# A two-layer graph network on one core: steps re-ordered, block sums a step later, layer 0's edges loaded 1 MB at a time

## The chip, the cores and the metric

The kernel runs on one core of a Trainium2 chip. The metric is the device time of one execution in microseconds (us); ten executions of the kernel before gave a median of 2218.96 us, from 2216.50 to 2221.39. Engines are named as the profile names them: PE (matrix multiply), PEld (its weight loads), DVE (vector), ACT (activations and copies), POOL (here: issues the gathers) and SP (here: issues most other transfers). SBUF is the on-chip memory; PSUM is the small memory in banks that PE writes its results to.

## The reference, cut to what matters

N = 6250 nodes, E = 106250 edges sorted by their destination, D = 256 features, all fp32. Both layers use the same `src`, `dst` and `edge_attr`.

```python
def layer_0(x, src, dst, edge_attr):
    msg = relu(x[src] + edge_attr)
    agg = segment_sum(msg, dst, num_segments=N)
    h = x + (x + agg)
    f = bn1(h)
    f = gelu(f @ W1.T + b1)
    f = f @ W2.T + b2
    return bn2(h + f)

def layer_1(x1, src, dst, edge_attr):
    h = gelu((x1[src] + edge_attr) @ W1m + b1m)
    agg = segment_sum(h @ W2m + b2m, dst, N) / maximum(deg, 1.0)
    u = gelu(agg @ W1u + b1u) @ W2u + b2u
    return layernorm(x1 + u, gamma, beta)

x1  = layernorm(x  + layer_0(x, ...))
out = layernorm(x1 + layer_1(x1, ...))
```

Each layer reads one row of 256 floats per edge from a table of nodes, at an address given by `src`, adds the edge's own row, applies a function, and sums the results by destination.

## The kernel before, in words

**Edges.** They are cut into 831 tiles of 128. Eight tiles make a *span* (104 spans; the last has seven tiles, the last of these ten edges). A span has two groups `g` of G = 4 tiles, a group two pairs of tiles that start at `q` = 0 and 2. A pair of 128 x 512 floats fills one PSUM bank.

**Nodes.** They are cut into 25 blocks of 256 (the last has 106). As edges are sorted by destination, a span touches one or two blocks. Blocks 22, 23 and 24 are complete after spans 98, 102 and 103.

**Layer 1 turned round.** (x1[src] + e) @ W1m + b1m is computed as proj[src] + e @ W1m, where proj = x1 @ W1m + b1m is made once per node. Layer 0 also computes z = e @ W1m for group 0 of each span and stores it in DRAM (`zst`, L1032 to L1041); layer 1 loads that and computes the product for group 1 alone. W2m @ W1u is joined to one matrix w12 (`join_weights`, L1056 to L1080).

**One span's way.** `load_edges` (L755) loads each group's 512 KB, three spans ahead (AHEAD). `gather` (L768, its transfer L772) issues eight indirect transfers on POOL, one per tile, into one of RING = 5 buffers `ring`. `lifted` (L804) copies two tiles of edges into a PSUM bank on ACT, and `add_to_gathered` (L816, DVE) adds them to the gathered rows. `activated` (L824, ACT) applies relu or gelu. `one_hots` (L833, DVE) makes 128 x 32 matrices of zeros and ones that say which of 32 consecutive node slots an edge belongs to; `into_slots` (L855, PE) multiplies by them, so that a span becomes 128 partial rows, and ACT copies these to `sums` (L861). `slot_nodes` (L842) makes the second matrix of zeros and ones, from slots to nodes, and `into_blocks` (L879, PE) adds the partial rows to the block's accumulator `acc`; in layer 0 it also counts the degrees, one matmul and one DVE addition for each block part (L886, L890). `turned` (L779) transposes two tiles of edges on PE into the one bank of the pool `eaP` (L785), and ACT copies them to `eaT` (L790); `product` (L793, PE L798) multiplies them by W1m.

**A block's way.** When its last span is in, a generator is started: `nodes_0` or `nodes_1`. Each step of the loop calls `advance` (L912), which lets every running generator do one more stage, up to its next `yield`. `nodes_0` (L918 to L987): scale and copy of acc (fT L924, hT L929); matmuls L935 and gelu L940; matmuls L948 and L953, additions L958 and L959, normalization (L898 to L905), store of x1; transposes L970 and copy L973; matmuls L979, addition L983 and the store of the block's rows of `proj`. `nodes_1` (L1082 to L1142): the mean by degree (L1086 to L1090), two stages of matmuls L1100 with L1105 and gelu L1109, then L1115 to L1136 with matmuls L1125, and the last normalization with the store of `out`.

**Order.** It is written out by hand; no scheduler moves anything. The engines run their own instruction streams in the order in which the code issues them, held only by data and buffers. `step_0(v)` and `step_1(v)` work on three spans at once: they gather span v, add and activate span u = v-1, and sum span w = v-2. SP issues the loads and stores, in order. PSUM has 8 banks: accP 2, slotP 1, eaP 1, workP 4, the last shared by lifted, product, degrees and nodes. Before the first gather, a check of `dst` computes `astray` (L751); POOL waits for it.

**Between the layers** stand the loads of layer 1's first three spans, the two last steps of layer 0, then `join_weights`, then the rest of the node stages; layer 1's first gather needs all of `proj`.

Of the kernel before, what the change touches and what calls it, by code (L numbers as in the profile page):

```python
# [17 lines left out]
G = 4  # L18
# [484 lines left out]
def kernel(  # L503
# [224 lines left out]
    with (  # L728
        tc.tile_pool(name="state", bufs=1) as state,
        tc.tile_pool(name="edges", bufs=(AHEAD + 1) * GROUPS) as ep,  # L730
# [4 lines left out]
        tc.tile_pool(name="eaP", bufs=1, space=bass.MemoryType.PSUM) as pse,  # L735
# [12 lines left out]

        ps = work()
# [5 lines left out]
        def load_edges(v, g):  # L755
            counts = tiles_of(v, g)
            ea = ep.tile([P, G, D], F32, name="ea")
            for j, k, n in runs(counts):
                r0 = (v * SPAN + g * G + j) * P
                nc.sync.dma_start(  # L760
                    out=ea[:n, j:k, :],
                    in_=edge_attr[r0 : r0 + (k - j - 1) * P + n, :].rearrange(
                        "(j p) d -> p j d", p=n
                    ),
                )
            return ea
# [12 lines left out]
        def turned(v, g, q, ea):  # L779

            pair = tiles_of(v, g)[q : q + 2]
            pe = pse.tile([P, 2, KC, P], F32, name="eaP")
            for j, n in enumerate(pair):
                for k in range(KC):
                    nc.tensor.transpose(  # L785
                        pe[:, j, k, :n], ea[:n, q + j, k * P : (k + 1) * P], ident[:n, :n]
                    )
            eaT = hp.tile([P, 2, KC, P], F32, name="eaT", bufs=3)
            for j, k, n in runs(pair):
                nc.scalar.copy(eaT[:, j:k, :, :n], pe[:, j:k, :, :n])  # L790
            return pair, eaT
# [55 lines left out]
        def into_slots(v, width):  # L847

            counts = tiles_of(v, 0) + tiles_of(v, 1)
            hot, r = hots.pop(v), rings[v % RING]  # L850
            ps = pss.tile([P, D + 1], F32, name="slotP")
            for i in range(PAIR):
                for j in range(i, len(counts), PAIR):
                    n, q = counts[j], j // PAIR
                    nc.tensor.matmul(  # L855
                        ps[q * SLOTS : (q + 1) * SLOTS, :width],
                        lhsT=hot[:n, j, :], rhs=r[:n, j, :width],
                        start=(i == 0), stop=(i == PAIR - 1 or j + 1 == len(counts)),
                    )
            sums[v] = hp.tile([P, D + 1], F32, name="sums")  # L860
            nc.scalar.copy(sums[v][:, :width], ps[:, :width])  # L861

        def into_blocks(v, acc, opened, degs=None):

            its, hot, lo0 = sums.pop(v), hot2s.pop(v), window[v][0]
            for b, lo, hi in parts(v):
                at, fresh = hot[:, lo - lo0 : hi - lo0], b not in acc
                begins = opened(b) if fresh else False
                if begins:

                    lo, hi = b * SB, b * SB + shape(b)[0]
                    at = hp.tile([P, SB], F32, name="hot3")[:, : hi - lo]
                    nc.vector.tensor_scalar(  # L873
                        at, ramp[:, : hi - lo], float(lo), node_of[:, v : v + 1],
                        op0=ALU.add, op1=ALU.is_equal,
                    )
                cols = slice(lo - b * SB, hi - b * SB)
# [6 lines left out]
                if degs is not None:  # L884
                    ps = work()
                    nc.tensor.matmul(  # L886
                        ps[:1, 0, : hi - lo], lhsT=its[:, D : D + 1], rhs=at,
                        start=True, stop=True,
                    )
                    nc.vector.tensor_add(degs[b][:, cols], degs[b][:, cols], ps[:1, 0, : hi - lo])  # L890
            return [b for b in sorted(acc) if last_span[b] == v]
# [20 lines left out]
        def advance():  # L912

            for gen in list(running):
                if next(gen, "done") == "done":
                    running.remove(gen)


        def nodes_0(b, acc, xb, deg):
# [11 lines left out]
            ps = work()  # L931
# [12 lines left out]
            ps = work()  # L944
# [14 lines left out]
            nc.vector.tensor_add(ps, ps, bn2_b[:n, None, :].to_broadcast([n, H, D]))  # L959
            x1 = npool.tile([P, SH, D], F32, name="x1")  # L960
            normalized(x1, ps, n, H)
# [3 lines left out]

            x1T = npool.tile([P, KC, SB], F32, name="x1T")
            ps = work()
# [8 lines left out]
            ps = work()  # L976
# [14 lines left out]
        def load_0(v):  # L991
            for b in range(blocks):
                if first_span[b] == v:
                    _, H, n = shape(b)
                    xbs[b] = npool.tile([P, SH, D], F32, name="xb", bufs=4)
                    nc.sync.dma_start(out=xbs[b][:n, :H, :], in_=rows_of(x, b))
            for g in range(GROUPS):
                eas[v, g] = load_edges(v, g)

        def opened_0(b):  # L1000
# [10 lines left out]
            degs[b] = npool.tile([1, SB], F32, name="degs", bufs=3)  # L1011
            nc.vector.memset(degs[b], 0.0)
            return False

        def step_0(v):
# [66 lines left out]
        def nodes_1(b, acc, x1, deg):  # L1082
# [13 lines left out]
            for i in range(0, UC, 2):  # L1096
                ps = work()
# [6 lines left out]
                for o in (i, i + 1):  # L1104
# [3 lines left out]
                    )  # L1108
                    nc.scalar.activation(  # L1109
# [4 lines left out]
            ps = work()  # L1114
# [7 lines left out]
            ps = work()  # L1122
# [6 lines left out]
            nc.vector.tensor_add(ps[:n, :H, :], ps[:n, :H, :], r[:n, :H, :])  # L1129
            mv = normalized(None, ps, n, H)  # L1130
            for h in range(H):
                nc.vector.scalar_tensor_tensor(
                    ps[:n, h, :], ps[:n, h, :], mv[:n, h, 0:1], row["L1_gnn_gamma"][:n, :],
# [3 lines left out]
                    ps[:n, h, :], ps[:n, h, :], mv[:n, h, 1:2], y[:n, h, :],  # L1137
                    op0=ALU.mult, op1=ALU.add,
                )
            yield  # L1140
            normalized(y, ps, n, H)
# [4 lines left out]
        def load_1(v):  # L1146
# [10 lines left out]
            eas[v, 0] = ep.tile([P, G, D], F32, name="ea")  # L1157
            nc.sync.dma_start(out=eas[v, 0].rearrange("p j d -> p (j d)"), in_=zst[v])
            eas[v, 1] = load_edges(v, 1)
# [4 lines left out]

        def step_1(v):
            u, w = v - 1, v - 2
# [4 lines left out]
            if 0 <= w:  # L1171
                slot_nodes(w)
            some = 0 <= u < V
            if some:
                first = turned(u, 1, 0, eas[u, 1])
                for q in (0, 2):
                    add_to_gathered(u, 0, q, lifted(u, 0, q, eas[u, 0]))
            if 0 <= w:
                into_slots(w, D)
            if some:  # L1180
                second = turned(u, 1, 2, eas[u, 1])
                add_to_gathered(u, 1, 0, product(*first))
                activated(u, 0, AF.Gelu)
                one_hots(u)
            full = into_blocks(w, acc_1, opened_1) if 0 <= w else []
            if some:
                add_to_gathered(u, 1, 2, product(*second))
                activated(u, 1, AF.Gelu)
            advance()
            for b in full:  # L1190
                gen = nodes_1(b, acc_1.pop(b), x1s.pop(b), degs_1.pop(b))
                next(gen)
                running.append(gen)
# [3 lines left out]
        for v in range(V):  # L1197
            step_0(v)
        for v in range(AHEAD):
            load_1(v)  # L1200
        step_0(V)
        step_0(V + 1)
        join_weights()
        while running:
            advance()
        for v in range(V + 2):
            step_1(v)
        while running:
            advance()
# [5 lines left out]

# [55 lines left out]
```

## Time and profile before

| what | value |
|---|---|
| median of 10 executions | 2218.96 us (2216.50 to 2221.39) |
| the profiled execution | 2217.28 us, its span 2215.4 us |
| PE, PEld busy | 1856.5 us (84%), 1452.1 us (66%) |
| DVE, ACT busy | 1440.3 us (65%), 1347.2 us (61%) |
| POOL busy | 1576.8 us (71%) |
| moved by DMA | 531.79 MB, mean 240 GB/s |

The page of the profile lists busy times, a picture of the span in 40 slices, the DMA queues, the chain of work that ended last, and the costliest groups of instructions. In a group's row the part behind the bar is the busy time, the mean of one instruction in ns, and the idle time of the engine just before these instructions with what ended most of it. In the waits a row reads: engine, tile and line, what it waited for, us in total, times, longest.

### The profile page before, as it was taken

To read this page: it belongs to the slowest core of one execution; us is meant where nothing else is said; L and a number is where in the kernel's file an instruction comes from. 1 tells how busy PE (TensorE), PEld (TensorE's weight loads), DVE (VectorE), ACT (ScalarE), POOL (GpSimd) and SP (SyncE) were. 2 spreads that over 40 slices of the span, in tenths; PEclk is the share of its full clock that TensorE was granted. 3 is DMA by queue.
4 is the path that set the end of the run, shared out by engine and by line. 5 is a ranking of instruction groups with operands and counts; after the bars stand their busy time and mean duration, and the time that the engine had idled before them with its cause. 6 is when DMAs were issued, how large, how long until landed. Compare 5 with 4: busy or idle time off the path is not lost.

```text
span 2215.4 us, 38426 instructions
## 1 busy us (share of the span) xinstructions
PE 1856.5 (84%) x11916; PEld 1452.1 (66%) x11916; DVE 1440.3 (65%) x4130; ACT 1347.2 (61%) x2143; POOL 1576.8 (71%) x1671
## 2 busy tenths in 40 slices
PE   3889989989899899889758878888888888888885
PEld 2667767767777777667546666666666666666664
DVE  4567666666666766667435676667667667666665
ACT  1566666666667666667534666566566566666664
POOL 3777777777777777777357777777777777777770
PEclk9999999999999999999879999999999999999998
DMA  7888988889889889888456677667667766776650
GB/s 231 267 276 281 286 276 284 278 283 288 274 280 291 277 274 292 279 274 272 147 179 226 213 226 235 224 213 241 215 218 230 236 214 215 240 231 211 221 183 19
DMA packets 313740, 531.79 MB, mean 240 GB/s; under 512 B 37989, under 2 KB 233144, under 8 KB 313400
## 3 DMA queue, kind: packets, MB, share of 16 engines
q1 hardware_dynamic: 231190, 307.82, 41.3%
q0 software_dynamic: 79744, 217.71, 33.3%
q10 hardware_dynamic: 2594, 3.71, 0.5%
q8 instruction: 100, 1.64, 0.3%
q14 instruction: 112, 0.92, 0.1%
HBM read 455.34 MB, written 73.75 MB: 239 GB/s over the span
## 4 chain that ended last, share of the span: by engine, by line
PE 22%; DVE 10%; ACT 7%; DMA 6%; issue 5%; POOL 1%; DVEq 0%; POOLq 0%
PE workP L798 11%; DMA ring<-proj,src_sb 6%; PE workP L1100 4%; PE acc L879 3%; ACT ring L824 3%; PE eaP L785 2%; ACT uT L1109 2%; DVE ring L816 2%; ACT eaT L790 2%; DVE hot L833 1%; DVE inv L1087 1%; DVE uT L1105 1%; POOL ring L772 1%; DVE stats L898 1%; PE slotP L855 1%
## 5 line engine op out<-in xcount | busy, mean ns | idle before, releaser
L772 POOL DMA_INDIRECT ring<-proj,src_sb x831 | 788.4, 949 | 299.2 <-issue 150.2
L772 POOL DMA_INDIRECT ring<-in_x_dram,src_sb x831 | 786.5, 946 | 286.0 <-issue 134.1
L798 PE MATMUL workP<-w1m_sb,eaT 128*128 128x256 f32 x3324 | 819.4, 391 | 7.6 <-DVE ring L816 6.4
L816 DVE TENSOR_TENSOR ring<-workP,ring 128x512 f32<-128x512 f32 x832 | 546.8, 685 | 429.2 <-ACT workP L809 157.3
L824 ACT ACTIVATE ring<-ring 128x1024 f32<-128x1024 f32 x418 | 439.6, 1052 | 553.1 <-DVE ring L816 453.9
L798 PEld LDWEIGHTS workP<-w1m_sb,eaT 128*128 128x128 f32 x3324 | 617.5, 195 | 102.1 <-DVE ring L816 17.2
L785 PE MATMUL eaP<-ident,ea 128*128 128x128 f32 x1662 | 266.2, 284 | 150.6 <-ACT eaT L790 150.4
L785 PEld LDWEIGHTS eaP<-ident,ea 128*128 128x128 f32 x1662 | 193.0, 143 | 263.7 <-ACT eaT L790 237.5
L809 ACT COPY workP<-ea 128x512 f32<-128x512 f32 x624 | 345.0, 589 | 0.0
L855 PE MATMUL slotP<-ring,hot 128*32 128x257 f32 (+1 forms) x3324 | 269.6, 390 | 62.7 <-ACT ring L824 41.7
L879 PE MATMUL acc<-hot,sums 128*128 128x160 f32 (+19 forms) x1360 | 227.3, 295 | 75.9 <-DVE hot L873 46.9
L790 ACT COPY eaT<-eaP 128x512 f32<-128x512 f32 x416 | 242.6, 583 | 63.9 <-PE eaP L785 62.8
L879 PEld LDWEIGHTS acc<-hot,sums 128*128 128x128 f32 x1360 | 203.7, 195 | 106.0 <-DVE hot L873 47.1
L833 DVE TENSOR_SCALAR hot<-ramp,slot 128x32 f32<-128x32 f32 x1662 | 266.9, 262 | 0.0
L855 PEld LDWEIGHTS slotP<-ring,hot 128*32 128x32 f32 x3324 | 109.6, 109 | 156.7 <-ACT ring L824 75.9
L1032 DVE COPY z<-workP 128x512 f32<-128x512 f32 x104 | 71.9, 691 | 90.8 <-PE workP L798 90.6
L900 ACT ACTIVATE mv<-mv,eps 128x2 f32<-128x2 f32 (+1 forms) x75 | 22.2, 295 | 136.6 <-DVE mv L899 136.3
L1100 PE MATMUL workP<-fT,w 128*128 128x256 f32 (+1 forms) x400 | 94.1, 379 | 0.7 <-DVE fT L1090 0.7
L900 ACT ACT_TABLE_LOAD x73 | 93.7, 1283 | 1.3
L1125 PE MATMUL workP<-w2u_sb,uT 128*128 128x256 f32 (+1 forms) x392 | 89.0, 379 | 3.4 <-ACT uT L1109 3.4
L1100 PEld LDWEIGHTS workP<-fT,w 128*128 128x128 f32 x400 | 76.0, 193 | 11.4 <-PE workP L1100 1.1
L1125 PEld LDWEIGHTS workP<-w2u_sb,uT 128*128 128x128 f32 (+1 forms) x392 | 74.1, 190 | 13.9 <-ACT uT L1109 3.8
(109 smaller groups left out, 1425.6 us busy)
## 6 DMA issues: line engine op xcount, KB each, us to landing
ea<-in_edge_attr_dram SPq DMA_DIRECT2D x310, 512.0 KB
zst<-z SPq DMA_DIRECT2D x104, 512.0 KB
ea<-zst SPq DMA_DIRECT2D x104, 512.0 KB
ring<-in_x_dram,src_sb POOLq DMA_INDIRECT x831
ring<-proj,src_sb POOLq DMA_INDIRECT x831
xb<-in_x_dram SPq DMA_DIRECT2D x24, 256.0 KB
x1d<-x SPq DMA_DIRECT2D x24, 256.0 KB
proj<-y SPq DMA_DIRECT2D x24, 256.0 KB
```

What stands on the lines that cost most here:

```text
L772: nc.gpsimd.indirect_dma_start(out=rings[v % RING][:n, g * G + j, :D], out_offset=None, in_=table, in_offset=bass.IndirectOffsetOnAxis(ap= ...
L785: nc.tensor.transpose(pe[:, j, k, :n], ea[:n, q + j, k * P : (k + 1) * P], ident[:n, :n])
L790: nc.scalar.copy(eaT[:, j:k, :, :n], pe[:, j:k, :, :n])
L798: nc.tensor.matmul(ph[:n, j, :], lhsT=eaT[:, j, k, :n], rhs=w1m_sb[:, k, :], start=(k == 0), stop=(k == KC - 1),)
L809: nc.scalar.copy(ps[:n, j:k, :], of[:n, q + j : q + k, :])
L816: nc.vector.tensor_add(r[:n, at + j : at + k, :D], ps[:n, j:k, :], r[:n, at + j : at + k, :D])
L824: nc.scalar.activation(at, at, func)
L833: nc.vector.tensor_scalar(hots[v][:n, j, :], ramp[:n, :SLOTS], slot[:n, t : t + 1], None, op0=ALU.is_equal,)
L855: nc.tensor.matmul(ps[q * SLOTS : (q + 1) * SLOTS, :width], lhsT=hot[:n, j, :], rhs=r[:n, j, :width], start=(i == 0), stop=(i == PAIR - 1 ...
L879: nc.tensor.matmul(acc[b][:, k, cols], lhsT=its[:, k * P : (k + 1) * P], rhs=at, start=(begins and k == 0), stop=(last_span[b] == v and k ...
L1100: nc.tensor.matmul(ps[:, o - i, :width], lhsT=w12[:, k, o * P : (o + 1) * P], rhs=mT[:, k, :width], start=(k == 0), stop=(k == KC - 1),)
L1125: nc.tensor.matmul(ps[:n, h, :], lhsT=uT[:, k, h * P : h * P + n], rhs=w2u_sb[:, k, :], start=(k == 0), stop=(k == UC - 1),)
```

## The change

Layer 0 loads a span's eight tiles of edges by one transfer of 1 MB into one tile; layer 1 loads z and group 1's edges into the two halves of such a tile. All transposes of a step stand together at its head, with the one-hot matrices, and use workP's banks; the pool eaP is gone. The activation of group 1 moves into the next step, the slots to a later place in the step, and the block sums from span v-2 to span v-3, at the step's head, so that each layer runs one step more. The degree sums of a span are one matmul into spare columns of slotP's bank. The node stages have a bank of their own (`nodeP`), more yields (five in nodes_0, six in nodes_1), and are advanced at two places of a step: the oldest generator early, the others late. The square roots of the normalizations stand in a stage of their own. `join_weights` moves from between the layers to the end of step 0.

```diff
-        tc.tile_pool(name="edges", bufs=(AHEAD + 1) * GROUPS) as ep,
+        tc.tile_pool(name="edges", bufs=AHEAD + 1) as ep,
-        tc.tile_pool(name="eaP", bufs=1, space=bass.MemoryType.PSUM) as pse,
+        tc.tile_pool(name="nodeP", bufs=1, space=bass.MemoryType.PSUM) as psn,
...
+        def edge_tiles(v):
+            ea = ep.tile([P, SPAN, D], F32, name="ea")
+            for g in range(GROUPS):
+                eas[v, g] = ea[:, g * G : (g + 1) * G, :]
             return ea
...
-            pe = pse.tile([P, 2, KC, P], F32, name="eaP")
+            pe = work().rearrange("p j (k e) -> p j k e", k=KC)
...
-            ps = pss.tile([P, D + 1], F32, name="slotP")
+            ps = pss.tile([P, 2 * D], F32, name="slotP")
...
+            if degs is not None:
+                span = window[v][1] - lo0
+                nc.tensor.matmul(
+                    rest[:, :span], lhsT=its[:, D : D + 1], rhs=hot[:, :span], start=True, stop=True
+                )
+                for b, lo, hi in parts(v):
+                    to = degs[b][:, lo - b * SB : hi - b * SB]
+                    nc.vector.tensor_add(to, to, rest[:, lo - lo0 : hi - lo0])
...
-            for g in range(GROUPS):
-                eas[v, g] = load_edges(v, g)
+            load_edges(v, range(GROUPS), edge_tiles(v))
...
         def step_0(v):
-            u, w = v - 1, v - 2
+            u, w, full = v - 1, v - 2, v - 3
             if v + AHEAD < V:
                 load_0(v + AHEAD)
             if v < V:
                 gather(v, x)
                 first = turned(v, 0, 0, eas[v, 0])
-                z = ep.tile([P, G, D], F32, name="z", bufs=2)
-            if 0 <= w:
-                slot_nodes(w)
+                second = turned(v, 0, 2, eas[v, 0])
+                zs[v] = ep.tile([P, G, D], F32, name="z", bufs=2)
             if 0 <= u < V:
-                for q in (0, 2):
-                    add_to_gathered(u, 0, q, lifted(u, 0, q, eas[u, 0]))
-            if 0 <= w:
-                into_slots(w, D + 1)
+                one_hots(u)
+            early, late = running[:1], running[1:]
+            if 0 <= full:
+                full_0(full)
+            if 0 <= w < V:
+                activated(w, 1, AF.Relu)
+            if 0 <= u < V:
+                add_to_gathered(u, 0, 0, lifted(u, 0, 0, eas[u, 0]))
+                add_to_gathered(u, 0, 2, lifted(u, 0, 2, eas[u, 0]))
+            advance(early)
             if v < V:
-                second = turned(v, 0, 2, eas[v, 0])
-                nc.vector.tensor_copy(z[:, 0:2, :], product(*first))
+                nc.vector.tensor_copy(zs[v][:, 0:2, :], product(*first))
             if 0 <= u < V:
-                activated(u, 0, AF.Relu)
                 for q in range(0, len(tiles_of(u, 1)), 2):
                     add_to_gathered(u, 1, q, lifted(u, 1, q, eas[u, 1]))
-                one_hots(u)
-            full = into_blocks(w, acc, opened_0, degs) if 0 <= w else []
+                activated(u, 0, AF.Relu)
+            if 0 <= w < V:
+                slot_nodes(w)
+                kept_slots(w, into_slots(w, D + 1))
             if v < V:
-                nc.vector.tensor_copy(z[:, 2:4, :], product(*second))
-                nc.sync.dma_start(out=zst[v], in_=z.rearrange("p j d -> p (j d)"))
-            if 0 <= u < V:
-                activated(u, 1, AF.Relu)
-            advance()
-            for b in full:
-                gen = nodes_0(b, acc.pop(b), xbs.pop(b), degs.pop(b))
-                next(gen)
-                running.append(gen)
+                nc.vector.tensor_copy(zs[v][:, 2:4, :], product(*second))
+                nc.sync.dma_start(out=zst[v], in_=zs.pop(v).rearrange("p j d -> p (j d)"))
+            advance(late)
...
         for v in range(V):
             step_0(v)
+            if v == 0:
+                join_weights()
         for v in range(AHEAD):
             load_1(v)
-        step_0(V)
-        step_0(V + 1)
-        join_weights()
-        while running:
-            advance()
-        for v in range(V + 2):
+        for v in range(V, V + 3):
+            step_0(v)
+        finish()
+        for v in range(V + 3):
             step_1(v)
-        while running:
-            advance()
+        finish()
```

`finish` advances all generators until none is left; `full_0` and `full_1` call `into_blocks` and start the generators of the blocks that it completes. `step_1` is re-ordered in the same way. In `nodes_0` and `nodes_1` every `work()` becomes `node_work()`, and `normalized` is split into `deviations`, `inverted` and `scaled`, with a yield before the square root.

More of the change, by code (lines that the diff above doesn't have):

```diff
@@ L747, in work, with node_work @@
             return psw.tile([P, 2, D], F32, name="workP")
+        def node_work():
+            return psn.tile([P, 2, D], F32, name="nodeP")
         ps = work()
@@ L910, with advance, finish, deviations @@
         running = []
-        def advance():
-            for gen in list(running):
+        def advance(which):
+            for gen in which:
                 if next(gen, "done") == "done":
                     running.remove(gen)
+        def finish():
+            while running:
+                advance(list(running))
+        def deviations(of, n, H):
+            stats = npool.tile([P, SH, 6], F32, name="stats")
+            mv = npool.tile([P, SH, 2], F32, name="mv", bufs=3)
+            for h in range(H):
+                nc.vector.bn_stats(stats[:n, h, :], of[:n, h, :])
+                nc.vector.bn_aggr(mv[:n, h, :], stats[:n, h, :])
+            return mv
+        def inverted(mv, n, H):
+            nc.scalar.activation(mv[:n, :H, 1], mv[:n, :H, 1], AF.Sqrt, bias=eps[:n, :])
+            nc.vector.reciprocal(mv[:n, :H, 1], mv[:n, :H, 1])
+        def scaled(to, of, mv, n, H):
+            for h in range(H):
+                nc.vector.tensor_scalar(
+                    to[:n, h, :], of[:n, h, :], mv[:n, h, 0:1], mv[:n, h, 1:2],
+                    op0=ALU.subtract, op1=ALU.mult,
+                )
         def nodes_0(b, acc, xb, deg):
@@ L930, in nodes_0 @@
             yield
-            ps = work()
+            ps = node_work()
             gT = npool.tile([P, KC, SB], F32, name="gT")
@@ L943, in nodes_0 @@
             yield
-            ps = work()
+            ps = node_work()
             for h in range(H):
@@ L975, in nodes_0 @@
             y = npool.tile([P, SH, D], F32, name="y")
-            ps = work()
+            ps = node_work()
             for h in range(H):
@@ L1096, in nodes_1 @@
             for i in range(0, UC, 2):
-                ps = work()
+                ps = node_work()
                 for o in (i, i + 1):
@@ L1108, in nodes_1 @@
                     )
+                for o in (i, i + 1):
                     nc.scalar.activation(
@@ L1113, in nodes_1 @@
                 yield
-            ps = work()
+            ps = node_work()
             nc.scalar.copy(ps[:n, :H, :], x1[:n, :H, :])
@@ L1121, in nodes_1 @@
                 )
-            ps = work()
+            yield
+            ps = node_work()
             for h in range(H):
@@ L1163, in opened_1, with full_1 @@
             return True
+        def full_1(v):
+            for b in into_blocks(v, acc_1, opened_1):
+                begun(b, nodes_1(b, acc_1.pop(b), x1s.pop(b), degs_1.pop(b)))
         def step_1(v):
-            u, w = v - 1, v - 2
+            u, w, full = v - 1, v - 2, v - 3
             if v + AHEAD < V:
@@ L1175, in step_1 @@
                 first = turned(u, 1, 0, eas[u, 1])
[L1176 to L1179, printed above, removed]
+                second = turned(u, 1, 2, eas[u, 1])
+                one_hots(u)
+            early, late = running[:1], running[1:]
+            if 0 <= full:
+                full_1(full)
+            if 0 <= w < V:
+                activated(w, 1, AF.Gelu)
             if some:
-                second = turned(u, 1, 2, eas[u, 1])
+                add_to_gathered(u, 0, 0, lifted(u, 0, 0, eas[u, 0]))
+                add_to_gathered(u, 0, 2, lifted(u, 0, 2, eas[u, 0]))
+            advance(early)
+            if some:
                 add_to_gathered(u, 1, 0, product(*first))
                 activated(u, 0, AF.Gelu)
-                one_hots(u)
-            full = into_blocks(w, acc_1, opened_1) if 0 <= w else []
+            if 0 <= w < V:
+                slot_nodes(w)
+                kept_slots(w, into_slots(w, D))
             if some:
                 add_to_gathered(u, 1, 2, product(*second))
-                activated(u, 1, AF.Gelu)
-            advance()
[L1190 to L1193, printed above, removed]
+            advance(late)
         for v in range(AHEAD):
```

67 lines of the change are left out of this document (37 added, 30 removed).

## The prediction

> **What bounds the kernel now.** I read the page's head and costliest groups, then the waits, then a table of busy time by stage, then the chain of waits where the layers meet, and last the timelines there and at the end. The groups come first:
>
> ```profile
> span 2215.4 us, 38426 instructions
> L772 POOL DMA_INDIRECT ring<-proj,src_sb x831 | 788.4, 949 | 299.2 <-issue 150.2
> L772 POOL DMA_INDIRECT ring<-in_x_dram,src_sb x831 | 786.5, 946 | 286.0 <-issue 134.1
> L785 PE MATMUL eaP<-ident,ea 128*128 128x128 f32 x1662 | 266.2, 284 | 150.6 <-ACT eaT L790 150.4
> ```
>
> PE is busy 84% of the span and POOL 71%, so PE looks like the bound. The waits speak against it:
>
> ```profile
> POOL ring L772 <- issue: 284.3, 933, 0.3
> POOL ring L772 <- DMA proj<-y: 46.4, 1, 46.4
> POOL ring L772 <- DMA ring<-in_x_dram,src_sb: 36.9, 121, 0.3
> POOL ring L772 <- DVE astray L751: 33.2, 1, 33.2
> POOL ring L772 <- PE slotP L855: 31.4, 103, 0.3
> ```
>
> POOL waits longer than 0.3 us exactly twice: at the start and between the layers. In between it issues one gather of 128 rows after another, 0.946 us busy and 0.30 us between, 1.25 us each; 831 x 1.25 = 1039 us in each layer. The 0.3 is the same whoever is named as releaser, so it is a cost of issuing. Stages, cut at POOL's restarts:
>
> ```profile
> 35.60:1075.00 1039.40, 940.31 (x6166) 730.72 (x6164) 701.14 (x2002) 679.82 (x1115) 786.52 (x831) 0.98 0.87 276
> 1075.00:1121.40 46.40, 34.44 (x152) 23.85 (x151) 11.54 (x34) 16.63 (x29) 0.02 (x2) 0.82 0.42 129
> 1121.40:2162.60 1041.20, 852.01 (x5452) 675.88 (x5452) 680.80 (x1955) 628.51 (x962) 788.35 (x831) 0.98 0.69 220
> 2162.60:2215.40 52.80, 27.13 (x144) 20.23 (x144) 30.95 (x90) 20.28 (x34) 0.00 (x0) 0.80 0.05 15
> ```
>
> The columns are length, then PE, weight loads, DVE, ACT and POOL busy, granted clock, DMA share and GB/s. A step (8 gathers) lasts 10.0 us. PE needs 940.3/104 = 9.04 of it in layer 0 and 8.19 in layer 1; DVE needs 6.7, ACT 6.5. So only four stages count: start 35.6, layer 0 1039.4, turn 46.4, layer 1 1041.2, tail 52.8, with 1.9 outside the span: the profiled run took 2217.28 us. The median, 2218.96, is 1.68 above that.
>
> The turn, from the last gather's landing to the last block of proj (pieces, in order; start, length):
>
> ```profile
> 1078.75 0.70 DVE ring L816
> 1079.59 3.75 PE workP L979 x8
> 1083.34 3.09 PE slotP L855 x14
> ...
> 1088.46 3.73 PE workP L935 x8
> ...
> 1094.24 3.70 PE workP L1068 x8
> 1097.94 1.68 PE workP L1076 x16
> 1099.62 0.97 PE workP L948 x4
> ...
> 1114.94 5.60 DMA proj<-y
> ```
>
> L979 is proj's matmul, L855 the slots, L935 and L948 the node MLP. L1064 to L1076 are join_weights, which needs nothing of layer 0 and stands on the path.
>
> **Loops.** Transposes together, in workP instead of the one eaP bank, take away most of the 150.4 us that PE waits for ACT's copies (L785). POOL waits for none of it: 0. The merged degree sums drop 170-104 = 66 matmuls and PSUM pairs in layer 0, 0.2 us each, 13 us of PE: 0. Activation and block sums a step later free a ring slot up to about 8 us later. Slot 45 was done at 504.3 and its next gather starts at 35.6+400x1.25 = 535.9, a slack of 31.6, so 23 remain: 0. That cover is gone if engine steps rise from 10.0 to over about 10.25 us for a whole layer (104 x 0.25 = 26). PE and DVE have the room.
>
> **The 1 MB load.** Layer 0 issues 104 fewer edge loads on SP; bytes and lines are the same, and they went out back to back before. They land over 20 us before use. Only the gathers behind them could suffer: a gather lands 5.75 us after issue, and each waits for the one eight earlier, 10.0 us back, a margin of 4.3. Cost 0.
>
> [...]
>
> **Start.** POOL waits 33.15 us for the bounds check (L751), which hangs on the load of dst, issued at 19.6 behind other loads that take turns on a few DMA semaphores. One load fewer per span moves this queue. An earlier first load gives -0.5. Bounds: dst can't be issued before about 16.4 (w2u issued at 13.0, 0.5 to the next issue, then 2.9 from b2m's issue at 16.7 to dst's), so -3.2; if 0.52 MB more of edges goes ahead of it at the 350 GB/s of that stretch, +1.5. I take -0.5, as most of the order is unchanged. join_weights, moved to just after step 0, stands behind step_0(0) on PE, ACT and DVE, 6.4 us on PE; step 1 is that late once, and the slack of three spans takes it: 0.
>
> **Turn.** Out of it goes join_weights: 1099.48-1093.05 = -6.4 (end of gelu L940 to start of L948). Into it comes one more step (blocks of spans 102 and 103 now follow the last adds) and a sixth stage of each block. PE was idle 1076.2 to 1079.6 and ran at a granted clock of 0.50 until 1092; eight matmuls took 3.75 us there and 1.89 at full clock. Walking the new order with half-clock durations: the last add at 1080.7 (second transposes and hots go first on PE and DVE) and hot2 0.3, so PE restarts at 1081.0; blocks(102) with degrees 2.9, transposes of block 22 1.1, slots 3.1: 1088.1; sums 0.4, blocks(103) 1.6: 1090.2 (0.1 of hand-over); projection of 22 (L979) 3.75: 1093.9; block 24's fT 0.77, hT 0.38, and y of 22 0.69, which the single nodeP bank puts ahead of block 23's matmuls: 1096.0; L935 1.9 and gelu 0.85: 1098.8. From there on 15.5 before, 16.3 now, since blocks 23 and 24 share one bank: last proj issued at 1115.1 to 1115.4, against 1114.94. I take +0.4. Bounds: clock full 3.0 us after the restart (as it was 3.0 us after 1106.3), -4; half clock through the later node matmuls as well (some 7 us of PE at full clock), +7.
>
> [...]
>
> **Tail.** The same DVE work lies behind the last add (2177.9): about 24 us of the 30.7 to the out DMA's issue. At full clock the new order ends where the old did, 2208.1. But PE now idles 3.9 us (2174.3 to 2178.2) and 5.4 us (2195.3 to 2200.7). The first puts eight matmuls of L1100 at half clock, 3.75-1.89 = +1.9; the second puts L1125 of the last block there, +1.5, of which DVE's lateness hides 0.9. Sum +2.5. Bounds: two table loads (1.28 each) leave the path with the split square roots, -2; half clock on all 13 us of PE in the tail where 6 to 7 were at full, +6.
>
> **Sum.** 2217.28 - 0.5 + 0.4 + 2.5 = 2219.7; with 1.68 the median is 2221.4. A difference of 0.2%, 4.4 us, is about what a measurement can tell from none, so "same" is 2214.5 to 2223.4.
>
> **Rivals.** *A, slower:* one nodeP bank makes each node stage wait for the reader of the stage before; PE then idles over 3 us between stages and runs at half clock through both drains. Turn +7, tail +6, start -0.5: 2217.28+12.5+1.68 = 2231.5. It decides once those idles pass about 3 us (loop idles of up to 2.6 us left the clock at 1.0). For: before already shows it twice (1106.3 to 1109.3 after an idle of 3.1). Against: the extra yields interleave blocks. *B, slower:* bursts of 1 MB push a gather's landing from 5.75 past 10.0 us, and POOL stalls: at 11 us, 10% of layer 0, +104, so 2323. For: DMA share is 0.87. Against: the loads were already back to back. *C, faster:* the clock recovers within 4 us of the restart (-4) and dst comes at its earliest (-3.2), tail even: 2217.28-7.2+1.68 = 2211.8. *D:* the loops gain from removed PE waits, as the change says on its face: POOL's 0.3 us would have to shrink; nothing in the profile lets it, so it has no chance of its own.
>
> **Chances.** Forecast 0.50 (own range 2217 to 2226: 0.44 within 0.2%, 0.06 above), A 0.28, B 0.05, C 0.17 (0.15 faster, 0.02 within). So faster 0.15, same 0.46, slower 0.39. The range 2212 to 2232 leaves out B, half of C and the upper part of A, together 0.2.
>
> **What would show it.** Right: POOL's waits again all 0.3 us but two, gathers 1.25 us, layers 1039 and 1041; PE's wait at the transposes far below 150 while the loop's length stays; nothing of join_weights after 1075 and a turn of 46 to 47 with half clock from its restart for 12 us; a tail near 55. Wrong: POOL waits of over 0.3 us inside a layer (B, or a full ring); a turn over 50 or a tail over 57 with clock 0.5 between node stages (A); a start below 33 or a turn below 43 (C).

## The result, and the profile after

The changed kernel takes 2229.51 us (median of 9 executions, 2225.99 to 2233.59), the kernel before 2218.40 (30 executions, 2214.23 to 2222.63). The ratio is 1.0048, 95% interval 1.0040 to 1.0057: slower by 11.1 us. The profiled execution took 2226.47 us, its span is 2224.7.

The page's span and its two groups of gathers (L772 is now L780):

```profile
span 2224.7 us, 37185 instructions
L780 POOL DMA_INDIRECT ring<-proj,src_sb x831 | 790.5, 951 | 304.1 <-issue 150.9
L780 POOL DMA_INDIRECT ring<-in_x_dram,src_sb x831 | 788.8, 949 | 285.7 <-issue 142.1
```

The waits of POOL:

```profile
POOL ring L780 <- issue: 293.0, 961, 0.3
POOL ring L780 <- DMA proj<-y: 51.0, 1, 51.0
POOL ring L780 <- DVE astray L754: 32.7, 1, 32.7
```

Again POOL waits longer than 0.3 us only twice, so the new loops do not hold it up. Busy time by stage, cut at POOL's restarts as before (length, PE, weight loads, DVE, ACT, POOL, granted clock, DMA share, GB/s):

```profile
35.10:1076.95 1041.85, 942.36 (x6056) 719.00 (x6054) 692.07 (x2008) 681.74 (x1118) 788.82 (x831) 0.96 0.84 275
1076.95:1127.95 51.00, 30.76 (x124) 21.22 (x124) 11.72 (x37) 12.41 (x25) 0.00 (x0) 0.77 0.36 115
1127.95:2171.50 1043.55, 884.00 (x5502) 685.67 (x5502) 676.42 (x1968) 630.81 (x969) 790.47 (x831) 0.95 0.69 220
2171.50:2224.70 53.20, 26.36 (x99) 18.80 (x98) 25.04 (x69) 13.90 (x26) 0.00 (x0) 0.73 0.04 14
```

Against before: start -0.5, layer 0 +2.4, turn +4.6, layer 1 +2.3, tail +0.4 (rounded), together +9.3 of span.

The turn from its first instructions, DVE and then PE, in the timeline (start, length, what; in brackets the idle time before and its releaser):

```profile
1083.74 0.69 DVE L824 TENSOR_TENSOR ring<-workP,ring 128x512 f32<-128x512 f32 x1 [6.38 <-DMA ring<-in_x_dram,src_sb]
```

```profile
1085.43 2.01 PE L891 MATMUL acc<-hot,sums 128*128 128x50 f32 x8 [8.85 <-DVE hot L850]
...
1099.63 2.78 PE L974 MATMUL nodeP<-fT,w1t_sb 128*128 128x256 f32 x8 [1.93 <-DVE y L1024]
```

The last full addition waits 6.38 us for its gather (3.77 before). PE idles 8.85 us, as the second one-hot matrix (L850) stands behind those additions on DVE. Block 23's first matmuls (L974) wait 1.93 us until DVE has read block 22's y out of the one nodeP bank. The clock granted in these stretches (columns as above):

```profile
1085.40:1097.20 11.80, 11.18 (x41) 6.62 (x42) 1.39 (x5) 2.79 (x6) 0.00 (x0) 0.50 0.35 124
1097.40:1100.60 3.20, 1.27 (x7) 0.87 (x6) 0.97 (x2) 2.06 (x3) 0.00 (x0) 1.00 0.02 9
1100.80:1107.40 6.60, 5.67 (x16) 4.13 (x16) 0.00 (x0) 0.84 (x2) 0.00 (x0) 0.50 0.07 25
1107.60:1121.80 14.20, 7.99 (x46) 6.08 (x46) 6.54 (x19) 3.36 (x8) 0.00 (x0) 1.00 0.14 46
```

Behind the idle 8.85 us PE runs at half clock (0.50) for some 12 us, though it is busy 11.18 us of 11.80. Then it is granted full clock (1.00), but waits 1.93 us for the bank and works only 1.27 us of 3.20; then half clock again (0.50) until about 1107.5.

### The profile page after: what moved, and what is told of

The parts are those of the page before. It is cut to its first block, busy times and chain, and to the rows that moved or that the text cites. A ratio compares the mean times of both kernels' runs of the same rounds, so it can differ in the third digit from the quotient of the medians.

```text
span 2224.7 us, 37185 instructions
## 1 busy us (share of the span) xinstructions
PE 1886.1 (85%) x11784; PEld 1446.1 (65%) x11784; DVE 1421.1 (64%) x4130; ACT 1340.8 (60%) x2139; POOL 1581.1 (71%) x1671
## 4 chain that ended last, share of the span: by engine, by line
PE 19%; DMA 14%; DVE 7%; issue 6%; ACT 4%; POOL 2%; DVEq 0%; ACTq 0%; POOLq 0%
DMA ring<-proj,src_sb 14%; PE workP L806 8%; PE acc L891 2%; PE nodeP L1177 2%; PE slotP L863 2%; POOL ring L780 2%; DVE ring L824 2%; PE nodeP L1150 2%; DVE hot L841 1%; ACT ring L832 1%; PE workP L793 1%; ACT eaT L798 1%; ACT workP L817 1%; ACT L947 1%; DVE uT L1155 1%
## 5 line engine op out<-in xcount | busy, mean ns | idle before, releaser
L780 POOL DMA_INDIRECT ring<-proj,src_sb x831 | 790.5, 951 | 304.1 <-issue 150.9
L780 POOL DMA_INDIRECT ring<-in_x_dram,src_sb x831 | 788.8, 949 | 285.7 <-issue 142.1
L806 PE MATMUL workP<-w1m_sb,eaT 128*128 128x256 f32 x3324 | 852.7, 402 | 75.9 <-DVE ring L824 53.4
L817 ACT COPY workP<-ea 128x512 f32<-128x512 f32 x624 | 343.5, 592 | 37.9 <-DVE ring L824 37.5
L798 ACT COPY eaT<-workP 128x512 f32<-128x512 f32 x416 | 224.2, 585 | 225.5 <-PE workP L793 224.5
L863 PE MATMUL slotP<-ring,hot 128*32 128x257 f32 (+1 forms) x3324 | 239.7, 393 | 6.1 <-ACT ring L832 5.5
L793 PE MATMUL workP<-ident,ea 128*128 128x128 f32 x1662 | 223.7, 277 | 13.1 <-DVE ring L824 12.5
L793 PEld LDWEIGHTS workP<-ident,ea 128*128 128x128 f32 x1662 | 196.9, 143 | 42.7 <-DVE ring L824 18.2
L872 ACT COPY sums<-slotP 128x257 f32<-128x257 f32 (+1 forms) x208 | 75.5, 363 | 119.1 <-PE slotP L863 118.5
L1150 PE MATMUL nodeP<-fT,w 128*128 128x256 f32 (+1 forms) x400 | 102.1, 401 | 35.7 <-DVE y L1191 30.8
L1160 ACT ACTIVATE uT<-uT,cols_sb 128x256 f32<-128x256 f32 (+1 forms) x100 | 44.8, 495 | 137.7 <-DVE uT L1155 137.7
L1150 PEld LDWEIGHTS nodeP<-fT,w 128*128 128x128 f32 x400 | 78.0, 203 | 54.7 <-DVE y L1191 34.4
L1177 PE MATMUL nodeP<-w2u_sb,uT 128*128 128x256 f32 (+1 forms) x392 | 92.0, 389 | 5.8 <-DVE y L1191 5.1
L1087 DVE COPY z<-workP 128x512 f32<-128x512 f32 x104 | 70.7, 680 | 29.5 <-PE workP L806 29.4
```

The source lines that it names most:

```text
L780: nc.gpsimd.indirect_dma_start(out=rings[v % RING][:n, g * G + j, :D], out_offset=None, in_=table, in_offset=bass.IndirectOffsetOnAxis(ap= ...
L793: nc.tensor.transpose(pe[:, j, k, :n], ea[:n, q + j, k * P : (k + 1) * P], ident[:n, :n])
L806: nc.tensor.matmul(ph[:n, j, :], lhsT=eaT[:, j, k, :n], rhs=w1m_sb[:, k, :], start=(k == 0), stop=(k == KC - 1),)
L817: nc.scalar.copy(ps[:n, j:k, :], of[:n, q + j : q + k, :])
L863: nc.tensor.matmul(ps[q * SLOTS : (q + 1) * SLOTS, :width], lhsT=hot[:n, j, :], rhs=r[:n, j, :width], start=(i == 0), stop=(i == PAIR - 1 ...
L1150: nc.tensor.matmul(ps[:, o - i, :width], lhsT=w12[:, k, o * P : (o + 1) * P], rhs=mT[:, k, :width], start=(k == 0), stop=(k == KC - 1),)
```

## Where the experiments ran

All twelve ran on four chips, one for each first letter of the labels. There the unchanged kernel before took 2778.35 (e), 2815.60 (f), 2819.61 (g) and 2820.46 us (h), not 2218. POOL did not set the pace, as it waited for ring slots. The waits of POOL in g3_before_join, which is the old order:

```profile
POOL ring L772 <- PE slotP L855: 567.8, 243, 11.6
```

The same wait was 31.4 us in 103 pieces of 0.3 in the first profile. So ratios measured there don't carry over to 2218 us. Stages can be compared where they begin at the last addition to the ring, since from there on no gather is waited for; the clock granted in them differs, and is given where it matters. The table gives, from the timelines of one profiled execution each: the first gather; layer 0 from there to the last addition; from the last addition to layer 1's first gather (the turn without the gather's landing); layer 1 to its last addition; from that to the end of the span.

| kernel | start | layer 0 | turn | layer 1 | tail | ratio, 95% interval |
|---|---|---|---|---|---|---|
| before, first profile | 35.6 | 1045.2 | 40.6 | 1056.5 | 37.5 | |
| after, first profile | 35.1 | 1050.0 | 42.9 | 1045.5 | 51.2 | 1.0048 (1.0040 to 1.0057) |
| e1_after | 35.6 | 1330.2 | 38.7 | 1355.6 | 51.5 | 1.0114 (1.0083 to 1.0145) |
| e2_late_loads | 35.9 | 1312.5 | 38.3 | 1361.2 | 51.5 | 1.0056 (1.0020 to 1.0091) |
| e3_drain_banks | 35.6 | 1315.0 | 33.3 | 1349.5 | 38.8 | 0.9994 (0.9963 to 1.0026) |
| e4_before_join | 35.8 | 1308.9 | 30.6 | 1378.3 | 37.7 | 0.9997 (0.9979 to 1.0015) |
| f1_before_join | 35.6 | 1322.4 | 29.6 | 1378.2 | 37.2 | 0.9983 (0.9964 to 1.0002) |
| f2_late_loads | 35.7 | 1313.3 | 44.9 | 1388.3 | 52.9 | 1.0165 (1.0125 to 1.0204) |
| f3_drain_banks | 35.2 | 1325.9 | 33.5 | 1402.6 | 37.8 | 1.0048 (1.0013 to 1.0083) |
| g1_mended | 35.1 | 1330.9 | 36.0 | 1424.8 | 37.9 | 1.0089 (1.0063 to 1.0115) |
| g2_before_1mb | 35.1 | 1314.2 | 37.4 | 1385.3 | 37.7 | 0.9991 (0.9976 to 1.0007) |
| g3_before_join | 35.8 | 1320.5 | 29.5 | 1393.5 | 38.0 | 0.9988 (0.9969 to 1.0007) |
| h1_join_1mb | 35.2 | 1323.4 | 30.7 | 1388.5 | 37.7 | 0.9985 (0.9970 to 1.0000) |
| h2_one_pool | 35.2 | 1341.1 | 35.9 | 1402.6 | 38.1 | 1.0082 (1.0054 to 1.0110) |

The tail column repeats to within 2 us for each kind of drain (37.2 to 38.0 in the old one, 51.2 to 52.9 with one bank, 37.8 to 38.8 with shared banks), which is why it may be read across the chips. The layers scatter by tens of microseconds.

## Experiments

**The changed kernel again (e1_after).** No edit.

> The changed kernel again, unchanged, beside the three others. Its profiled layers were 1041.85 and 1043.55 us long against 1039.40 and 1041.20 before, 1.254 us a gather against 1.251. Theory 'change': the new order makes each gather's issue slower, so this run shows 1.254 again while the kernel with the old order in this call (e4_before_join) shows 1.251. Rival 'chip': the 3 ns belong to the chip or the moment; both kernels show the same interval here. Turn 51 us and tail 53 us in either case, ratio to before 1.004 to 1.006.

Neither the 51 us of the turn nor the ratio could be tested, as the layers took 27 to 30% longer than in the first profile of after. The gather interval could: I take the mean from start to start of gathers that did not wait (under 1.265 us). It was 1.250 in the first profile of before and 1.253 in that of after. Here it was 1.252 in e1_after, 1.250 in e2_late_loads (the same loops on the same chip) and 1.252 in e4_before_join, the old order; in the f runs 1.250 (f1, old order), 1.250 (f2) and 1.253 (f3, both new). In the g and h runs it was the other way round: 1.253 in g2, g3 and h1 (old order), 1.250 in g1 and h2 (new order). It differs between executions by as much as the 3 ns and doesn't follow the order. "Change" falls; the 4.7 us in the two layers can't be put down to the change. Of the rival, the chip falls too, since the interval varies on one chip; that it belongs to the moment is left, without a cause.

**Layer 1's first loads later (e2_late_loads, f2_late_loads).**

```diff
-        for v in range(AHEAD):
-            load_1(v)
         for v in range(V, V + 3):
             step_0(v)
+        for v in range(AHEAD):
+            load_1(v)
         finish()
```

> Changed kernel, but the loads of layer 1's first three spans (3 MB) are issued behind the last three steps of layer 0 instead of ahead of them. Theory 'collision': the last gather landed after 8.51 us, not 5.75, because those loads were issued from 1073.9 on, 2 us ahead of it; without them it lands in 5 to 6 us, PE restarts 3 us earlier, and the turn falls from 51 to 47 or 48; ratio to before 1.0025 to 1.004. Rival 'order': the landing is late for another reason, or the time is lost again in the half clock; turn 50 to 51, ratio 1.005.

> Changed kernel with the loads of layer 1's first three spans behind the last steps of layer 0, measured again at 1.25 us a gather. Theory 'collision': last gather lands in 5 to 6 us instead of 8.5, turn 51 to 47 or 48, ratio to before 1.0025 to 1.004 (the changed kernel: 1.0048). Rival 'order': the landing stays at 8 us, or the clock takes the gain back; turn 50 to 51, ratio 1.0045 to 1.005. Gather interval 1.254 if it belongs to the new order, 1.251 if it belongs to the chip.

Inconclusive both times. In the first profile of after the first of these loads of edges is issued 0.7 us ahead of the last gather (before: 0.9 behind it), but where PE lags, it comes 26 us behind it (e1_after), so that there is no collision to remove. Turns of 38.3 and 44.9 show no gain. Whether the collision made the landing late, 2.4 us of the 4.6, stays open.

**Node stages of the drains in workP's banks (e3_drain_banks, f3_drain_banks).** `draining` is filled before the steps from V on, in each layer, and emptied between the layers.

```diff
         def node_work():
+            if draining:
+                return work()
             return psn.tile([P, 2, D], F32, name="nodeP")
```

> Changed kernel, but in the two drains (the steps from V on and what follows) the node stages take their PSUM banks from workP's four, not from the one bank nodeP. Theory 'one bank' (rival A of the prediction): stages of two blocks that waited for each other's readers now overlap, PE idles less; turn 51 to 47 or 48, tail 53 to 50 or 51, ratio 1.002 to 1.003. Rival: the chain goes through one block's own stages and the late restart; turn and tail change by under 1 us, ratio 1.004 to 1.005.

> Changed kernel with the node stages of both drains in workP's four banks instead of nodeP's one, measured again at 1.25 us a gather. Theory 'one bank': turn 51 to 47 or 48, tail 53 to 50 or 51, ratio 1.002 to 1.003. Rival 'late restart': turn and tail change by under 1 us, ratio 1.004 to 1.005.

The turn falls from 38.7 (e1, same chip) to 33.3 and from 44.9 (f2, same chip, with late loads as well) to 33.5; the tail from 51.5 to 38.8 and from 52.9 to 37.8. "One bank" is shown, and in the tail it is far larger than I expected. In the turn e1 and e3 were granted nearly the same clock (0.87 and 0.85), f2 and f3 not (0.70 and 0.85), so 5.4 is the cleaner reading there. PE's timeline in the tail of e1_after:

```profile
2770.65 3.75 PE L1150 MATMUL nodeP<-fT,w 128*128 128x256 f32 x8 [3.17 <-DVE y L1191]
2775.36 3.78 PE L1150 MATMUL nodeP<-fT,w 128*128 128x256 f32 x8 [0.96 <-DVE uT L1155]
2780.11 1.14 PE L1150 MATMUL nodeP<-fT,w 128*128 128x106 f32 x8 [0.96 <-DVE uT L1155]
2784.22 2.04 PE L1150 MATMUL nodeP<-fT,w 128*128 128x106 f32 x8 [2.97 <-DVE y L1170]
2787.01 5.22 PE L1177 MATMUL nodeP<-w2u_sb,uT 128*128 128x256 f32 x16 [0.74 <-DVE uT L1155]
2797.27 3.46 PE L1177 MATMUL nodeP<-w2u_sb,uT 128*106 128x256 f32 x8 [5.05 <-DVE y L1191]
```

and of e3_drain_banks (lines moved by 4):

```profile
2740.57 4.52 PE L1154 MATMUL workP<-fT,w 128*128 128x256 f32 x24
2745.64 1.14 PE L1154 MATMUL workP<-fT,w 128*128 128x106 f32 x8 [0.55 <-DVE uT L1159]
2749.64 8.00 PE L1181 MATMUL workP<-w2u_sb,uT 128*128 128x256 f32 x24 [2.86 <-ACT uT L1164]
```

With one bank each of six groups waits until DVE has read the group before, often of the other block: 13.85 us of idle time in the brackets. With four banks the same work stands in three groups with 3.41 us. The timeline of the first profile of after has the same six groups with the same waits (3.18, 0.97, 0.97, 2.97, 0.75, 5.05), so they are in it too.

With fewer waits the granted clock was higher too, as rival A had it. In the tail the same 98 matmuls keep PE busy 26.16 us at a granted 0.72 in e1, 20.26 us at 0.78 in e3. In e3's turn PE keeps full clock once it has it:

```profile
1362.40:1384.00 21.60, 15.79 (x83) 12.43 (x81) 8.60 (x27) 8.36 (x16) 0.02 (x1) 1.00 0.32 94
```

In f3 it does too, with the same 0.85 over the turn; in g1 and h2, two runs with shared banks that follow below, it falls once more for some 3 us (0.76 over the turn in both). With one bank it falls to half right behind the wait of 1.93 us for y (L974) in the first profile of after, in e1 and in f2 (0.50 from 1100.8, 1377.2 and 1364.1), but in e2 only behind later waits of 1.67 and 1.92 us (0.50 from 1371.6). That this one wait makes it fall is therefore not shown.

**The kernel before with join_weights at step 0 (e4_before_join, f1_before_join, g3_before_join).**

```diff
         for v in range(V):
             step_0(v)
+            if v == 0:
+                join_weights()
...
         step_0(V + 1)
-        join_weights()
```

> Kernel before with one edit: join_weights moved from between the layers to the end of step 0, as in the change. If its 6.4 us stood on the path as the chain of waits showed, turn 46.4 to 40 or 41 us, nothing elsewhere, ratio to before 0.997. If something else was late by as much (DVE's or ACT's stages of blocks 23 and 24), turn 44 to 46, ratio 0.999 to 1.0. If step 0 with it delays the first ring slots, a wait of POOL above 0.3 us shows in the first 100 us.

> Kernel before with join_weights at the end of step 0, as e4_before_join, measured again, since in that run the layers took 25% longer (POOL waited 531 us for slots) and no term of the turn could be read. If the layers go at 1.25 us a gather: turn 46.4 to 40 or 41 us, ratio 0.997, if the join stood on the path; turn 44 to 46 and ratio 0.999 to 1.0 if other work was late by as much. Gather interval: 1.251 if the 3 ns of the changed kernel belong to its order.

> Kernel before with join_weights after step 0, the third time, for a reading at 1.25 us a gather: turn 46.4 to 40 or 41, ratio 0.997. If PE lags POOL again: 30 us from the last addition to the restart (e4 30.6, f1 29.6), ratio 0.998 to 1.0.

The turn is 30.6, 29.6 and 29.5 us. The nearest partner is g2_before_1mb, on the same chip as g3, with the join in its old place and the 1 MB load: 37.4, so the join is worth 7.9 there. PE's timeline in g2 (lines moved by 6 and 7):

```profile
1355.89 1.99 PE L942 MATMUL workP<-fT,w1t_sb 128*128 128x256 f32 x8
...
1359.95 3.70 PE L1074 MATMUL workP<-w1u_sb,fT 128*128 128x512 f32 x8 [1.63 <-ACT fT L1070]
...
1365.19 1.11 PE L955 MATMUL workP<-w2s_sb,gT 128*128 128x256 f32 x4
```

and in g3:

```profile
1361.23 1.99 PE L935 MATMUL workP<-fT,w1t_sb 128*128 128x256 f32 x8
1363.79 1.13 PE L948 MATMUL workP<-w2s_sb,gT 128*128 128x256 f32 x4 [0.56 <-ACT gT L940]
```

From the first node matmuls to the second it is 9.30 us with the join between and 2.56 without, 6.7 of the 7.9. The three ratios lie at 0.998 to 1.000, each interval reaching 1: a gain of up to 0.2% fits, and is not settled. The turn of 40 us at 1.25 us a gather could not be measured.

**The 1 MB load alone (g2_before_1mb).** The kernel before with the span's tile in one piece:

```diff
-            for g in range(GROUPS):
-                eas[v, g] = load_edges(v, g)
+            load_edges(v, range(GROUPS), edge_tiles(v))
```

> Kernel before with the 1 MB edge load of layer 0 alone (the tile of a span in one piece, in layer 1 two loads into it). The prediction: SP's issues lie off the path, cost 0 in the loops, and the start 0.5 us earlier; ratio 0.9995 to 1.0005, first gather at 35.1. Rival B: bursts push the gathers' landing out, POOL waits over 0.3 us in layer 0, ratio above 1.002. [...]

First gather at 35.13 (g3, same chip: 35.81), ratio 0.9991 with 1 inside the interval: no cost to be seen. The earlier start is less certain than it looks: over all profiles it is 35.1 to 35.9 with the 1 MB load and 35.6 to 35.8 without. Layer 0 took 1314.2 us against 1320.5 of g3, which is within the scatter. Rival B is excluded by the first profile of after, where no gather in layer 0 waits longer than 0.3 us.

**Both mends (g1_mended).** The edits of e2 and e3 together.

> Changed kernel with both mends: node stages of the drains in workP's banks, and layer 1's first loads behind layer 0's last steps. From the end of the last addition to the first gather of layer 1 the changed kernel took 42.9 us in its first profile and 38.7 in e1_after, with the banks of workP 33.4 and 33.5 (e3, f3). Theory 'one bank': 33 to 37 us here. If the layers go at 1.25 us a gather, the last gather also lands in 5 to 6 us, the turn is 44 to 45, and the ratio 1.000 to 1.002; if PE lags POOL, as in the six runs so far, only the 33 to 34 shows. Rival 'late restart': 38 us or more.

36.0 in the turn (at a granted clock of 0.76) and 37.9 in the tail, as "one bank" had it. The ratio, 1.0089, is still above 1: here it lies in the layers (1330.9 and 1424.8 against 1314.2 and 1385.3 of g2, though the profiled execution of g1 took 2866.80 us, 20 more than its median).

**The two useful parts (h1_join_1mb).** The edits of g2 and g3 together.

> Kernel before with the two parts of the change that looked useful alone: join_weights after step 0 and the 1 MB edge load. If both terms are as read so far (about 7 us less from the last addition to the restart, against g2_before_1mb's 37.4; start 0.5 us earlier) and the layers are untouched: 29 to 31 us from the last addition to the restart, first gather at 35.1, ratio 0.997 to 0.999. Rival: the gain goes into the layers' scatter; ratio 0.999 to 1.001.

Turn 30.7, start 35.2, ratio 0.9985 with an interval that ends at 1.0000. This is the only version whose interval lies nowhere above the kernel before.

**No separate bank at all (h2_one_pool).**

```diff
-        tc.tile_pool(name="nodeP", bufs=1, space=bass.MemoryType.PSUM) as psn,
-        tc.tile_pool(name="workP", bufs=4, space=bass.MemoryType.PSUM) as psw,
+        tc.tile_pool(name="workP", bufs=5, space=bass.MemoryType.PSUM) as psw,
...
         def node_work():
-            return psn.tile([P, 2, D], F32, name="nodeP")
+            return work()
```

> Changed kernel without the bank of its own for the node stages: workP has five banks and everything takes from them, in the loops too. Theory 'one bank': from the last addition to the restart 33 to 36 us (changed kernel 38.7 and 42.9), from the last addition to the end 38 (51.2 and 51.5); what is left against the kernel before in the layers belongs to the order of the steps; ratio to before 1.000 to 1.006 where PE lags POOL, 0.997 to 1.000 where the layers go at 1.25 us a gather. Rival 'the bank keeps the loops apart': the layers get longer than the changed kernel's by 10 us or more, since node stages then hold banks that lifted, turned and product wait for; ratio over 1.01.

The drains are mended (35.9, again at a granted clock of 0.76, and 38.1), the ratio is 1.0082. Layers of 1341.1 and 1402.6 stand against 1323.4 and 1388.5 of h1 on the same chip, +31.8. Layer 0 is longer than in any other run, as the rival had it, but g1, which keeps nodeP in the loops, loses 56.2 in both layers against g2, some 36 if its slow execution is allowed for. So there the layers lose without the separate bank about as they do with it; the bank is not what makes that loss, and which part of the new order does was not found. At the first profiles' pace POOL sets the layers: in after its waits there are all 0.3 us, and the layers are 4.7 us longer than before.

## Why the prediction was right and where it was wrong

The range held the time, and the likeliest case did not come: the median is 2229.5, 8.1 above 2221.4 and 2 below rival A's 2231.5. A's place, the one nodeP bank, is shown, and so are the waits between the node stages (13.85 us in the tail of e1, 3.41 in e3) and a lower clock with them (0.72 against 0.78). Its price of +7 in the turn and +6 in the tail is not how the sum came about, and its condition was too strict: the prediction has idle times of up to 2.6 us leave the clock at 1.0, but already in the first profile of before an idle time of 2.10 us (to 177.65) is followed by 0.50 from 177.6 to 180.8. Of the signs that the prediction gave for A, a turn over 50 us came (51.0) and a tail over 57 did not (53.2).

- **Loops: right in mechanism.** POOL's waits in the layers are all 0.3 us. The layers are 4.7 us longer all the same, since a gather took 1.253 instead of 1.250 us; the experiments show such a difference between executions whatever the order. No step of the sum had a term for it.
- **1 MB load and start: right.** 0 and -0.5 predicted; -0.5 in the profile, -0.7 in g2 against g3. The start scatters by as much (35.1 to 35.9 with the 1 MB load), so this term is not proven.
- **Join: right, a little low.** 6.4 predicted; 7.9 measured in g2 against g3, 6.7 of it between the two groups of node matmuls.
- **Turn: wrong by 4.2.** The sum said +0.4, the profile shows +4.6. Two terms failed. The restart of PE: "the last add at 1080.7" and a restart at 1081.0, 6.0 us after POOL's last gather was issued through; it came 8.5 after it (1085.43-1076.95), as the last gather landed later: 2.5. And the walk from the restart to the last proj, 34.1 to 34.4 predicted, 36.3 measured (1085.43 to 1121.75). The 12 us of half clock came as predicted (0.50 from 1085.4 to 1097.2); what the walk did not have is that the clock falls a second time, for 6.6 us and more (0.50 from 1100.8 to 1107.4), right behind the wait for y in the one bank. PE is busy 5.67 us there at 0.50, by an estimate from that 2.8 more than at full clock. The term "16.3 now, since blocks 23 and 24 share one bank" put 0.8 on the bank and 0.7 on the y of 22; e3 gives 5.4 for it, f3 11.4 with a difference in clock.
- **Tail: near in sum, by luck.** +2.5 predicted, +0.4 measured. "The same DVE work lies behind the last add (2177.9)" failed. The last addition ends 16.2 us after the last gather's issue began (2161.72) before, and 2.9 us after it (2170.60) in the new order, 13.3 nearer:

```profile
2177.48 0.41 DVE L816 TENSOR_TENSOR ring<-workP,ring 10x256 f32<-10x256 f32 x1
```

```profile
2173.04 0.41 DVE L824 TENSOR_TENSOR ring<-workP,ring 10x256 f32<-10x256 f32 x1
```

  More DVE work is left behind it: 23.6 us busy, 20.4 before (the prediction said about 24). And the drain from there is 13.7 longer (51.2, 37.5 before), of which e3 puts 12.7 on the one bank. That the two nearly cancel was not foreseen; it is where a gain went that I had not seen.
- **What stays open.** The medians differ by 11.1. Turn, tail and start explain 4.5 of it; the 4.7 of the layers in this pair of profiles is not shown to come from the change, and what the other executions spent it on was not profiled. Among the executions of the changed kernel, 2225.99 us came with a mean granted clock of 0.952 and 2232.99 with 0.940, which would fit drains that get the half clock for longer or shorter; but the longest, 2233.59, had 0.947, and it was not tested.

By an estimate from the first measurement and the differences of e3 to e1, the changed kernel with workP's banks in the drains would take 2229.5-5.4-12.7 = 2211.4 us at the first profiles' pace. It was not measured there.

## What to carry to other kernels

When one queue paces the loops, as POOL did here with waits of 0.3 us alone, cost engine work in the loops at nothing and walk the drains instruction by instruction: there the buffers that a loop hides are on the path (the one bank took 12.7 us of the tail by e3). A bank that is enough for one stage a step can be a chain of waits when two blocks drain together (13.85 us of idle PE in e1, 3.41 in e3); let the drain borrow the loop's idle banks. And look at where the last piece of the loop's work ends, not only at what follows: here the re-ordering moved it 13.3 us nearer to the last gather's issue in layer 1.

## What of the hardware was not expected

After 8.85 us without work PE was granted half clock (0.50) from 1085.4 to 1097.2, while it was busy 11.18 us of 11.80. Half clock also came behind shorter idle times than the prediction's 3 us: 2.10 us in the first profile of before (0.50 from 177.6 to 180.8), though not each time (2.10 us in the same profile left it at 1.00 from 256.6 to 259.1, and 1.93 us in e2 from 1358.0 to 1371.3).

In g2_before_1mb, g3_before_join and f1_before_join DVE starts some copies late. In g2, the second product of a step ends at 803.88 on PE, by the profile, which models the ends of matmuls. Its copy on DVE starts 4.5 us later, only after PE's slot matmuls (L862), which it doesn't need:

```profile
801.91 1.97 PE L805 MATMUL workP<-w1m_sb,eaT 128*128 128x256 f32 x8
...
807.64 0.38 PE L862 MATMUL slotP<-ring,hot 128*32 128x257 f32 x1 [0.60 <-issue]
```

```profile
808.40 0.69 DVE L1046 COPY z<-workP 128x512 f32<-128x512 f32 x1 [4.06 <-PE slotP L862]
```

In g2 this copy's line waits 77.2 us in 24 pieces for the slots, in g3 73.4 us in 25 and in f1 83.8 us in 33; in the first profile of before (L1040) it waits only 8.6 us in 15, all for its own product. The cause was not found, nor is it shown that this is what makes the same kernel 25 to 27% slower on the four chips of the experiments. A change that costs 0.5% at one pace cost 1.1% at the other (e1_after).
